# Expert tiles of a mixture-of-experts layer: whole tiles of one expert first, the remainders in quarters of tiles on TensorE column groups

## The chip, the core and the metric

The kernel runs on one core of a Trainium2 chip. A core has TensorE (PE in the profile, with its weight loads as PEld), VectorE (DVE), ScalarE (ACT), GpSimd (POOL) and SyncE (SP, which issues most DMAs). The metric is the device time of one execution in microseconds. The kernel before took 489.15 us (median of 12 runs, 488.44 to 491.28).

## What is computed

A layer norm of x [2, 2048, 256] feeds two branches, whose sum is added to x. One is an RWKV-like attention: two projections, a scan over time per channel, an output projection. The other is a mixture of experts: every one of the 4096 tokens goes through a shared expert of width 512 and through the two of eight experts (width 256) that its gate scores highest. All is f32.

```
xn = layernorm(x)
scores = softmax(xn @ gate_w.T + gate_b);  top_w, top_i = top_k(scores, 2)
expert_e(t) = (silu(t @ w1[e].T + b1[e]) * (t @ w3[e].T + b3[e])) @ w2[e].T + b2[e]
y = sum over the 2 chosen e of top_w * expert_e(xn)
z = (silu(xn @ ws1.T + bs1) * (xn @ ws3.T + bs3)) @ ws2.T + bs2
out = x + attention(xn) + y + z
```

## The kernel before

There are 8 chunks of 512 tokens. For each chunk the kernel loads x and norms it (`norm_flow`: statistics on DVE, 1/std on POOL at lines 459 and 460, the scaling on DVE or ACT), turns it on PE (`turn_flow`) and takes the gate's logits (`by_e`, line 502). These logits are computed by four matmuls with 32 weight columns each, one for each 128 tokens; each writes its own 32 partitions of one PSUM bank.

`route_flow` then picks the two experts of each token and gives each of the 8192 (token, expert) pairs a slot: the pairs of an expert stand together, and each expert's stretch is rounded up to whole tiles of 128 slots. Eight experts round up by less than 8 tiles together, so 64 + 7 = 71 tiles are always enough, and 71 are always computed. `scatter_flow` writes the normed rows to their slots in DRAM (`xs_d`) with 64 indirect DMAs from POOL's queue (line 661); before that the whole of `xs_d` is cleared by 18 DMAs (line 426), so that unused slots carry a target out of bounds. Every second scatter also waits for a PE product (`keep_pace`): the one that was planned `PACE` = 4000 ns before it.

A tile (`tile_flow`) then does: the rows are read back in pairs of tiles (line 966, four DMAs) and turned by DVE (line 970); `ph` = rows times w1 and w3 of the tile's expert, 512 columns, two matmuls over the 256 input channels (line 1006); DVE adds the bias (line 1019), ACT takes the silu (line 1024), DVE multiplies (line 1026), PE turns the result (line 1032) and ACT copies it out of PSUM (line 1036); `pos` = that times w2, 256 columns, two matmuls (line 1042); DVE adds b2 (line 1046), and POOL scatters the rows to `ys_d` (line 1051). The expert's number is read from `owner` into a register of PE and of DVE (`find`, line 951), and weights `we` and biases `b13`, `b2` are addressed with it. At the end `collect_flow` reads `ys_d` back and adds the two weighted rows of each token (line 1080).

The other work of PE is the shared expert (`hidden_flow`, line 856; `dense_flow`, line 924) and the attention's projections (`wvp`, `wrp`, line 796). The attention's exponentials (line 759) and the silu of the tiles take different ACT tables, and ACT loads one at each change.

The order of all this is not left to a scheduler: every piece is a Python generator that says how long it expects to hold which engine (`yield on(400, "POOL")`), which events it needs and which rooms (counted buffers) it takes. `Plan.run` plays these against each other once, when the program is built, and emits the instructions in the order that comes out. The chip then runs each engine's instructions strictly in that order, with semaphores between engines. The numbers in `on(...)` cost nothing on the chip; they decide the order alone. `U` is a pool of 32 buffers of 2 KB per partition.

Of the kernel before, what the change touches and what calls it, by code (L numbers as in the profile page):

```python
# [29 lines left out]
F32 = mybir.dt.float32  # L32
# [8 lines left out]
P = 128  # L41
# [154 lines left out]

TILES = 2 * B * T // P + E - 1

# [6 lines left out]

Q = 32

PIECES = (((0,), (1,), (2,), (3,)), ((0, 1), (2, 3)))
NU = 32
KEEP = 3  # L210

PACE = 4000

# [12 lines left out]
def rwkv_moe_kernel(  # L226
# [36 lines left out]
    XST, SIS, HST, Y = Room(plan, 2), Room(plan, 3), Room(plan, 3), Room(plan, 3)  # L263
    STATS = Room(plan, 3)
    ONE = {}
# [21 lines left out]
    part_d = nc.dram_tensor("part_d", [B * T, C], F32, kind="Internal").ap()  # L287
    bias_d = nc.dram_tensor("bias_d", [2 * E * NI, P], F32, kind="Internal").ap()
    xs_d = nc.dram_tensor("xs_d", [TILES * P, R], F32, kind="Internal").ap()

# [33 lines left out]
    def constants():  # L324
        make_identity(nc, ident)
        nc.gpsimd.memset(zero, 0.0)
        nc.gpsimd.memset(neg_half, -0.5)
        nc.gpsimd.memset(ones, 1.0)

        nc.gpsimd.memset(before, 1.0)  # L330
        nc.gpsimd.affine_select(
            out=before, in_=before, pattern=[[1, P]], compare_op=ALU.is_gt, fill=0.0, base=0, channel_multiplier=-1
        )

        for e in range(E):
            nc.gpsimd.memset(rev[:, e : e + 1], float(E - e))

        nc.gpsimd.iota(starts, pattern=[[P, TILES]], base=0, channel_multiplier=0, allow_small_or_imprecise_dtypes=True)
        nc.gpsimd.memset(wg[:, :, E:], 0.0)
        nc.gpsimd.memset(st_pp, -10000.0)  # L340
        nc.gpsimd.memset(st_bb, 0.0)
        nc.gpsimd.memset(st_aa, 0.0)
# [40 lines left out]
    def load_flow():  # L383
# [38 lines left out]
        nc.gpsimd.memset(none[:, :, R_TO], float(4 * B * T))  # L422
        for j in range(0, TILES, NT):
            n = min(NT, TILES - j)
            yield on(900, "SP")
            nc.sync.dma_start(
                xs_d[j * P : (j + n) * P, :].rearrange("(p n) c -> p n c", p=P), none[:, :n, :]
            )
        land(TILES * P * 1024, [have["cleared"]], X)

# [13 lines left out]
    def norm_flow(c, groups):  # L444
# [12 lines left out]
        rstd = two.tile([P, m], F32, tag="rstd", name=f"rstd_{of}")  # L457
        yield on(400, "POOL")
        nc.gpsimd.tensor_scalar(rstd, mv[:, :, 1], EPS, None, ALU.add)
# [68 lines left out]
    def route_flow():  # L528
# [71 lines left out]

        room_i = pool.tile([P, E], I32, tag="room_i", name="room_i")
        nc.vector.tensor_scalar(room_i, each[:, 0, :], float(P - 1), None, ALU.add)
        nc.vector.tensor_scalar(room_i, room_i, 7, 7, ALU.logical_shift_right, ALU.logical_shift_left)
        room = small("room")
        nc.vector.tensor_copy(room, room_i)
        end = small("end")
        nc.vector.tensor_tensor_scan(end, room, zero.to_broadcast([P, E]), 0.0, ALU.add, ALU.add)

        off = small("off")
        nc.vector.tensor_tensor(off, end, room, ALU.subtract)  # L610
        nc.vector.tensor_tensor(off, off, each[:, 1, :], ALU.add)
        nc.vector.tensor_tensor(off, off, upto[:, 2, :], ALU.subtract)
        nc.vector.tensor_tensor(off, off, each[:, 2, :], ALU.add)
        nc.vector.tensor_scalar(off, off, -1.0, None, ALU.add)
        nc.vector.tensor_tensor(run, run, off.unsqueeze(2).to_broadcast([P, E, G]), ALU.add)
        for n, (which, to) in enumerate(zip((one1, one2), slot)):
            yield on(1250, "DVE")
            nc.vector.tensor_tensor(eq, which, run.rearrange("p e g -> p g e"), ALU.mult)
            nc.vector.tensor_reduce(q, eq, AX.X, ALU.add)
            nc.vector.tensor_copy(to, q)  # L620
        have["routed"].set()

        yield on(1700, "DVE")
        past = pool.tile([P, TILES, E], F32, tag="past", name="past")
        nc.vector.tensor_tensor(
            past, end.unsqueeze(1).to_broadcast([P, TILES, E]),
            starts.unsqueeze(2).to_broadcast([P, TILES, E]), ALU.is_le,
        )
        count = small("count", (P, TILES))
        nc.vector.tensor_reduce(count, past, AX.X, ALU.add)  # L630
        nc.vector.tensor_scalar(owner, count, float(E - 1), None, ALU.min)
        nc.vector.tensor_scalar(likes, count, float(E - 1), None, ALU.min)
        nc.vector.tensor_scalar(likes, likes, -1.0, float(E), ALU.mult, ALU.add)
# [15 lines left out]
    def scatter_flow():  # L649
# [5 lines left out]
        for side, chunks in (("left", LEFT), ("right", RIGHT)):  # L655
            for c in chunks:
                for n in range(NT):
                    g = c * NT + n
                    for w in range(2):
                        yield on(1340, "POOL")  # L660
                        step = nc.gpsimd.indirect_dma_start(  # L661
                            out=xs_views[2 * g + w],
                            out_offset=bass.IndirectOffsetOnAxis(ap=slot[w][:, g : g + 1], axis=0),
                            in_=xn[c][:, n, :],
                            in_offset=None,
                        )
                        if w:
                            keep_pace(step)
                land(0, [scattered[c]])
# [6 lines left out]
            else:  # L676
                late["pool3"] = ctx.enter_context(tc.tile_pool(name="late3", bufs=3, side="right"))
                late["poolg"] = ctx.enter_context(tc.tile_pool(name="lateg", bufs=3, side="right"))
        for j in range(TILES):
            plan.add(tile_flow(j), 10 + j / 100)  # L680
        for j in range(0, TILES, 2):
            plan.add(rows_flow(j), 10 + j / 100)
        for j in range(0, TILES, GO):
# [4 lines left out]
    def bias_rows_flow():  # L688
# [8 lines left out]
        yield on(400, "SP")  # L697
        nc.sync.dma_start(bias_d, bt)
        land(0, [have["bias_d"]], U)

    def bias_flow():
        for c in LEFT:
            yield scattered[c]
        yield have["bias_d"]
        for m in range(2):
            yield on(2600, "SP")
            part = bias_d[ts(m, E * NI), :].rearrange("(e i) p -> e (i p)", e=E)
            nc.sync.dma_start(late["b13"][:, :, m, :], part.partition_broadcast(P))
        yield on(2600, "SP")
        nc.sync.dma_start(late["b2"], b_out[:E, :].partition_broadcast(P))  # L710
        land(P * E * 3 * C * 4, [have["bias"]])
# [131 lines left out]
    def hidden_flow(c, i):  # L843
# [3 lines left out]
        if c in LAST:  # L847
            yield turn[TILES - 5]
        pts = []
# [92 lines left out]

    rows_in = {j: event() for j in range(0, TILES, 2)}
    gone = {j: event() for j in range(0, TILES, GO)}
    turned_rows, stored = {}, [0]

    which = {}

    def find(j):

        which[j] = nc.values_load(
            owner[0:1, j : j + 1], engines=[ENG.PE, ENG.DVE], min_val=0, max_val=E - 1,
            skip_runtime_bounds_check_because="a count of experts, held to the last one",
        )

    def rows_flow(j):


        for c in range(NCH):
            yield scattered[c]  # L960
        n = min(2, TILES - j)
        yield on(1500, "SP", (U, 1), (ROWS, 1))
# [4 lines left out]
        yield 3000  # L967
        yield on(620, "DVE", (U, 1), (XST, 1))
        xT = u([P, n, NC, P], f"xsT_{j}")
# [23 lines left out]
    def tile_flow(j):  # L993
        j0 = j // 2 * 2
        yield rows_in[j0]
        xT = turned_rows[j0][0][:, j % 2]
        yield have["we"]
        if j:
            yield turn[j - 1]
        yield on(1740, "PE", (PS, 1), (PH, 1), spare=(PS, 1))  # L1000
        if j == 0:
            find(j)
        ev = which.pop(j)
        ph = bank([P, 2, I], f"ph_{j}")
        for k in range(NC):
            nc.tensor.matmul(  # L1006
                ph, xT[:, k, :], we[:, bass.ds(ev, 1), 0:2, k, :], start=(k == 0), stop=(k == NC - 1)
            )
        if j + 1 < TILES:
            find(j + 1)  # L1010
        turned_rows[j0][1] -= 1
        if turned_rows[j0][1] == 0:
            U.give()
            XST.give()
        turn[j].set()
        yield have["bias"]
        yield on(690, "DVE", (U, 1), (H, 1))
        h = u([P, 2, I], f"h_{j}")
        nc.vector.tensor_tensor(h, ph, late["b13"][:, bass.ds(ev, 1), :, :], ALU.add)  # L1019
        PS.give()  # L1020
# [17 lines left out]
        HP.give()  # L1038
        yield on(880, "PE", (PS, 1), (PO, 1), spare=(PS, 1))
        po = bank([P, C], f"pos_{j}")  # L1040
        for i in range(NI):
            nc.tensor.matmul(po, hT[:, i, :], we[:, bass.ds(ev, 1), 2, i, :], start=(i == 0), stop=(i == NI - 1))  # L1042
        HST.give()
        yield on(420, "DVE", (U, 1), (YS, 1))
        y = u([P, C], f"ys_{j}")
        nc.vector.tensor_tensor(y, po, late["b2"][:, bass.ds(ev, 1), :], ALU.add)  # L1046
        PS.give()
# [180 lines left out]
```

## Time and profile before

| what | value |
|---|---|
| median of 12 runs | 489.15 us |
| the profiled execution: time | 489.38 us |
| the profiled execution: span in the trace | 487.4 us |
| granted TensorE clock over it | 0.995 |
| DVE busy | 394.2 us (81%) |
| ACT busy | 186.9 us (38%) |
| POOL busy | 168.4 us (35%) |
| DMA moved | 77.36 MB, 159 GB/s in the mean |

The page gives busy time for each engine over the span, the chain of work that ended last, and the costliest groups of instructions, with the mean time of one and the idle time ahead of it. A matmul of f32 stands in the trace as two records. The records of matmuls overlap (one shows 595 ns for 512 columns while the next starts 430 ns later), so durations of matmuls are read from the distance of starts and not from the busy time.

### The profile page before, as it was taken

To read this page: it belongs to the slowest core of one execution; us is meant where nothing else is said; L and a number is where in the kernel's file an instruction comes from. 1 tells how busy PE (TensorE), PEld (TensorE's weight loads), DVE (VectorE), ACT (ScalarE), POOL (GpSimd) and SP (SyncE) were. 2 spreads that over 40 slices of the span, in tenths; PEclk is the share of its full clock that TensorE was granted. 3 is DMA by queue.
4 is the path that set the end of the run, shared out by engine and by line. 5 is a ranking of instruction groups with operands and counts; after the bars stand their busy time and mean duration, and the time that the engine had idled before them with its cause. 6 is when DMAs were issued, how large, how long until landed. Compare 5 with 4: busy or idle time off the path is not lost.

```text
span 487.4 us, 6242 instructions
## 1 busy us (share of the span) xinstructions
PE 470.0 (96%) x1683; PEld 278.5 (57%) x1683; DVE 394.2 (81%) x783; ACT 186.9 (38%) x332; POOL 168.4 (35%) x205
## 2 busy tenths in 40 slices
PE   3999999999999899999999999999999999999996
PEld 1555566445776455555655555656555555444885
DVE  4776999887695798999799779997699866978793
ACT  3776311531500166224912295224922277211000
POOL 6540057777785041433223331442233232000000
PEclk9999999999999899999999999999999999999999
DMA  6999998829345777234322432228321210388872
GB/s 206 370 395 402 219 208 326 264 104 341 137 139 178 97 145 160 75 78 102 71 65 76 117 75 65 82 61 217 76 56 48 75 65 2 106 266 267 270 243 101
DMA packets 92097, 77.36 MB, mean 159 GB/s; under 512 B 52989, under 2 KB 79774, under 8 KB 91808
## 3 DMA queue, kind: packets, MB, share of 16 engines
q1 hardware_dynamic: 85584, 60.12, 45.0%
q0 software_dynamic: 6480, 16.85, 9.7%
q8 instruction: 15, 0.25, 0.2%
q14 instruction: 18, 0.15, 0.1%
HBM read 42.31 MB, written 35.54 MB: 160 GB/s over the span
## 4 chain that ended last, share of the span: by engine, by line
PE 75%; ACT 9%; DVE 8%; issue 3%; POOL 2%; DMA 1%; DVEq 0%; SPq 0%; POOLq 0%
PE p L856 20%; PE ph L1006 16%; PE po L924 15%; PE pos L1042 9%; PE wvp L796 6%; PE wrp L796 5%; ACT L1024 3%; ACT L759 3%; PE hsp L1032 2%; POOL rstd L460 2%; DVE h L1019 1%; DVE aa L811 1%; ACT sis L1024 1%; DVE ys L1046 1%; DVE stats L454 1%
## 5 line engine op out<-in xcount | busy, mean ns | idle before, releaser
L1051 POOL DMA_INDIRECT ys_d<-ys,goes x71 | 77.3, 1089 | 186.1 <-DVE ys L1046 164.4
L1006 PE MATMUL ph<-we,xsT 128*128 x284 | 134.7, 599 | 2.2 <-issue 2.2
L856 PE MATMUL p<-xnT,ws 128*128 128x512 f32 x256 | 114.4, 595 | 0.2 <-DMA ws<-in_w_sh_dram 0.2
L661 POOL DMA_INDIRECT xs_d<-xn,slot x64 | 71.1, 1111 | 49.4 <-DMA we<-in_w_exp_dram 27.8
L856 PEld LDWEIGHTS p<-xnT,ws 128*128 128x128 f32 x256 | 48.0, 191 | 55.2 <-issue 51.9
L1006 PEld LDWEIGHTS ph<-we,xsT 128*128 128x128 f32 x284 | 50.7, 192 | 40.9 <-issue 40.0
L1042 PEld LDWEIGHTS pos<-we,hsT 128*128 128x128 f32 x284 | 53.5, 190 | 31.3 <-issue 19.3
L1042 PE MATMUL pos<-we,hsT 128*128 x284 | 70.2, 381 | 0.8 <-ACT hsT L1036 0.8
L1019 DVE TENSOR_TENSOR h<-ph,b 128x512 f32<-128x512 f32 x71 | 48.6, 687 | 15.0 <-PE ph L1006 13.8
L924 PE MATMUL po<-ws,si 128*128 128x256 f32 x256 | 59.2, 379 | 0.0
L1024 ACT ACTIVATE sis<-h 128x256 f32<-128x256 f32 x71 | 29.0, 415 | 70.9 <-DVE h L1019 70.6
L924 PEld LDWEIGHTS po<-ws,si 128*128 128x128 f32 x256 | 48.6, 190 | 10.4 <-issue 3.6
L863 ACT ACTIVATE si<-p,vec 128x512 f32<-128x512 f32 x32 | 21.5, 684 | 60.0 <-PE p L856 60.0
L1036 ACT COPY hsT<-hsp 128x256 f32<-128x256 f32 x71 | 24.4, 368 | 47.5 <-PE hsp L1032 47.5
L1026 DVE TENSOR_TENSOR sis<-sis,h 128x256 f32<-128x256 f32 x71 | 29.1, 414 | 10.8 <-ACT sis L1024 10.5
L1046 DVE TENSOR_TENSOR ys<-pos,b 128x256 f32<-128x256 f32 x71 | 28.6, 414 | 8.1 <-PE pos L1042 5.3
L924 PE MATMUL po<-wo,rw 128*128 128x256 f32 x128 | 31.9, 379 | 0.0
L824 ACT ACTIVATE th<-wrp 128x512 f32<-128x512 f32 x16 | 9.6, 598 | 57.1 <-PE wrp L796 57.1
L796 PE MATMUL wrp<-xnT,wr 128*128 128x512 f32 x64 | 30.1, 592 | 0.0
L970 DVE STREAM_TRANSPOSE xsT<-xs 128x512 f32<-128x512 f32 (+1 forms) x36 | 25.0, 696 | 5.2 <-DMA xs<-xs_d 4.9
L796 PE MATMUL wvp<-xnT,wv 128*128 128x512 f32 x64 | 29.0, 593 | 0.0
L924 PEld LDWEIGHTS po<-wo,rw 128*128 128x128 f32 x128 | 24.3, 190 | 5.9 <-issue 2.6
(128 smaller groups left out, 525.7 us busy)
## 6 DMA issues: line engine op xcount, KB each, us to landing
xs<-xs_d SPq DMA_DIRECT2D x140, 64.0 KB, 2.4
xs_d<-none SPq DMA_DIRECT2D x17, 516.0 KB, 10.4
y<-ys_d SPq DMA_DIRECT2D x32, 256.0 KB, 3.4
xb<-in_x_dram SPq DMA_DIRECT2D x8, 512.0 KB, 4.6
we<-in_w_exp_dram SPq DMA_DIRECT2D x16, 256.0 KB, 10.9
pa<-part_d SPq DMA_DIRECT2D x8, 512.0 KB, 4.7
xn<-in_x_dram SPq DMA_DIRECT2D x14, 256.0 KB, 6.7
part_d<-xb SPq DMA_DIRECT2D x5, 512.0 KB, 3.1
```

The source lines that it names most:

```text
L661: step = nc.gpsimd.indirect_dma_start(out=xs_views[2 * g + w], out_offset=bass.IndirectOffsetOnAxis(ap=slot[w][:, g : g + 1], axis=0), in_ ...
L796: nc.tensor.matmul(pt, wa[name][:, k, ts(ch, P)], xnT[c][k], start=(k == 0), stop=(k == NC - 1))
L856: nc.tensor.matmul(pt, ws13[:, m, k, ts(i, P)], xnT[c][k], start=(k == 0), stop=(k == NC - 1))
L924: nc.tensor.matmul(po[:, j, :], l[:, ts(2 * half + j, P)], r, start=(i == 0), stop=(i == len(parts) - 1))
L970: nc.vector.transpose(xT.rearrange("p n k (b t) -> p n b k t", t=Q), t.rearrange("p (n b) (k i) -> p n b k i", n=n, i=Q))
L1006: nc.tensor.matmul(ph, xT[:, k, :], we[:, bass.ds(ev, 1), 0:2, k, :], start=(k == 0), stop=(k == NC - 1))
L1019: nc.vector.tensor_tensor(h, ph, late["b13"][:, bass.ds(ev, 1), :, :], ALU.add)
L1024: nc.scalar.activation(si, h[:, 0, :], AF.Silu)
L1026: nc.vector.tensor_tensor(si, si, h[:, 1, :], ALU.mult)
L1042: nc.tensor.matmul(po, hT[:, i, :], we[:, bass.ds(ev, 1), 2, i, :], start=(i == 0), stop=(i == NI - 1))
L1046: nc.vector.tensor_tensor(y, po, late["b2"][:, bass.ds(ev, 1), :], ALU.add)
L1051: nc.gpsimd.indirect_dma_start(out=ys_views[j], out_offset=bass.IndirectOffsetOnAxis(ap=goes[:, j : j + 1], axis=0), in_=y, in_offset=None ...
```

## The change

The slots are given out in another way. Each expert first gets its whole tiles: the number of its pairs divided by 128, rounded down. Those of all experts come first. What is left of each expert (under 128 pairs) is rounded up to quarters of a tile (32 slots), and these follow, expert after expert. The first 57 tiles (`UNI`) then can be done like before, as tiles that belong to one expert. The last 9 are `mixed`: each quarter of 32 rows has an expert of its own. Together 66 tiles, not 71.

A mixed tile runs its matmuls per quarter: 32 weight columns (32 rows of the tile), 512 or 256 moving columns, each quarter into its own 32 partitions of the bank, four matmuls where there was one. The moving weights of a quarter are first copied by ACT from `we` to a buffer of its own (`own`, 2 x 512 elements per quarter for w1 and w3, 1 x 512 for w2: 12 copies a tile, 108 in all), with the expert's number in an ACT register (4 loads a tile). The biases are gathered by row with two indirect DMAs from POOL's queue a tile. The mixed tiles do not come last: they are put in at places 20, 25, ... 60 of the order (`SEQ`).

Other edits: routing computes the two sets of stretches (13 more small DVE instructions ahead of the slots, some of 256 elements); only the mixed part of `xs_d` is cleared (3 DMAs, not 18); `bias_d` is laid out by expert; rows of uniform tiles are still read in pairs, of mixed tiles singly; and four planned costs change: the scatter 1340 to 1290, the norm's POOL step 400 to 950 + 150 per group of 128 rows, `PACE` 4000 to 2000, and a planned pause of 5000 ahead of the tiles. 

The core of the diff:

```diff
-TILES = 2 * B * T // P + E - 1
+Q = 32
+PAIRS = 2 * B * T
+UNI = PAIRS // P - (E - 1)
+TILES = -(-(PAIRS // Q + E - 1) // (P // Q))
+START, EVERY = 20, 5
+SEQ = list(range(UNI))
+for m in range(UNI, TILES):
+    SEQ.insert(START + EVERY * (m - UNI), m)
+AT = {j: n for n, j in enumerate(SEQ)}
+TOGETHER = {j: min(2, UNI - j) if j < UNI else 1 for j in [*range(0, UNI, 2), *range(UNI, TILES)]}
-PACE = 4000
+PACE = 2000
...
-        for j in range(0, TILES, NT):
+        for j in range(UNI, TILES, NT):
             n = min(NT, TILES - j)
             yield on(900, "SP")
             nc.sync.dma_start(
                 xs_d[j * P : (j + n) * P, :].rearrange("(p n) c -> p n c", p=P), none[:, :n, :]
...
-        yield on(400, "POOL")
+        yield on(950 + 150 * m, "POOL")
...
+        room_i = pool.tile([P, 2, E], I32, tag="room_i", name="room_i")
+        nc.vector.tensor_copy(room_i[:, 0, :], each[:, 0, :])
+        nc.vector.tensor_scalar(room_i[:, 0, :], room_i[:, 0, :], 7, 7, ALU.logical_shift_right, ALU.logical_shift_left)
+        nc.vector.tensor_copy(room[:, 0, :], room_i[:, 0, :])
+        nc.vector.scalar_tensor_tensor(room_i[:, 1, :], each[:, 0, :], float(Q - 1), room[:, 0, :], ALU.add, ALU.subtract)
+        nc.vector.tensor_scalar(room_i[:, 1, :], room_i[:, 1, :], 5, 5, ALU.logical_shift_right, ALU.logical_shift_left)
...
         nc.vector.tensor_tensor(run, run, off.unsqueeze(2).to_broadcast([P, E, G]), ALU.add)
+        nc.vector.tensor_tensor(both, run, end[:, 0, :].unsqueeze(2).to_broadcast([P, E, G]), ALU.is_ge)
+        nc.vector.tensor_tensor(both, both, further.unsqueeze(2).to_broadcast([P, E, G]), ALU.mult)
+        nc.vector.tensor_tensor(run, run, both, ALU.add)
...
-                        yield on(1340, "POOL")
+                        yield on(1290, "POOL")
...
-        for j in range(TILES):
-            plan.add(tile_flow(j), 10 + j / 100)
+        yield 5000
+        for j in SEQ:
+            plan.add(tile_flow(j), 10 + AT[j] / 100)
...
+    def expert(j, q, engines):
+        return nc.values_load(
+            owner[q * Q : q * Q + 1, j : j + 1], engines=engines, min_val=0, max_val=E - 1, ...
+    def find(n):
+        if n < TILES and SEQ[n] < UNI:
+            which[SEQ[n]] = expert(SEQ[n], 0, [ENG.PE, ENG.DVE])
+
+    def quarters_flow(j):
+        yield have["bias_d"]
+        yield have["we"]
+        yield turn[SEQ[AT[j] - 6]]
...
+        yield on(1300, "POOL", (MIX, 1), (U, NC * len(quarters) + 1), spare=(U, 2))
+        biases("b13", bias_d, 2 * I)
+        for q in quarters:
+            for k in range(NC):
+                yield on(650, "ACT")
+                if k == 0:
+                    which[j, q] = bass.ds(expert(j, q, [ENG.Activation]), 1)
+                mine[q, k] = u([P, 2, I], f"own_{j}_{q}_{k}")
+                nc.scalar.copy(mine[q, k], we[:, which[j, q], 0:2, k, :])
+        own_in[j].set()
+        yield turn[j]
+        MIX.give()
+        yield on(1300, "POOL", (U, len(quarters) + 1), spare=(U, 2))
+        biases("b2", b_out[:E, :], C)
+        for q in quarters:
+            yield on(650, "ACT")
+            mine[q] = u([P, NI, C], f"own2_{j}_{q}")
+            nc.scalar.copy(mine[q], we[:, which[j, q], 2, :, :])
+        own2_in[j].set()
...
         for k in range(NC):
-            nc.tensor.matmul(
-                ph, xT[:, k, :], we[:, bass.ds(ev, 1), 0:2, k, :], start=(k == 0), stop=(k == NC - 1)
-            )
+            for q in range(P // Q) if mixed else ():
+                rows_q = ts(q, Q)
+                nc.tensor.matmul(
+                    ph[rows_q], xT[:, k, rows_q], own[j][q, k], start=(k == 0), stop=(k == NC - 1)
+                )
+            if not mixed:
+                nc.tensor.matmul(ph, xT[:, k, :], we[:, e, 0:2, k, :], start=(k == 0), stop=(k == NC - 1))
```

The second product of a mixed tile (`pos`) is cut into quarters in the same way, and its two bias adds read the gathered rows.

## The prediction

> **What bounds the kernel now.** I read the page's busy times first, then the chain of waits, then the costliest groups.
>
> ```profile
> span 487.4 us, 6242 instructions
> ...
> PE 470.0 (96%) x1683; PEld 278.5 (57%) x1683; DVE 394.2 (81%) x783; ACT 186.9 (38%) x332; POOL 168.4 (35%) x205
> ...
> PE 75%; ACT 9%; DVE 8%; issue 3%; POOL 2%; DMA 1%; DVEq 0%; SPq 0%; POOLq 0%
> ```
>
> PE is busy 96% of the span, and three quarters of the chain that ended last is PE. The 17 us without PE lie in few places: 6 ahead of the first matmul, some 3 up to 15 us (waits for weights), about 1 at 26 us, 2.2 ahead of the first tile, six times about 0.5 where ACT changes between exponentials and silu, and 4 at the end. So the time is PE's stream plus these gaps, and each part of the change is priced as stream or as gap.
>
> What a tile costs is read from starts, in PE's timeline at 203 us (start, duration, engine, line, tiles, count):
>
> ```profile
> 203.81 1.88 PE L1006 MATMUL ph<-we,xsT 128*128 x4
> 205.53 1.03 PE L1042 MATMUL pos<-we,hsT 128*128 x4
> 206.40 0.38 PE L1032 MATMUL hsp<-ident,sis 128*128 128x128 f32 x2
> 206.62 1.88 PE L1006 MATMUL ph<-we,xsT 128*128 x4
> ```
>
> Four records of 512 columns take 205.53 − 203.81 = 1.72 us (0.43 each), pos 0.87, hsp 0.22: from ph to ph 2.81 us.
>
> **1. Five tiles fewer.** 5 × 2.81 = **−14.0**. Their DVE work (5 × 1.86 = 9.3 us), scatters and loads go too, beside PE, for nothing.
>
> **2. Column groups.** A mixed tile gives four products of 32 columns for each one of 128. If they run one after another, ph and pos cost four times as much; if abreast, the same. The row that shows it is by_e, whose four matmuls also have 32 columns each:
>
> ```profile
> 18.25 1.88 PE L856 MATMUL p<-xnT,ws 128*128 128x512 f32 x4
> 20.06 0.64 PE L502 MATMUL by_e<-xnT,wg 128*32 128x128 f32 x16
> 20.64 3.70 PE L856 MATMUL p<-xnT,ws 128*128 128x512 f32 x8
> ...
> 41.07 1.08 PE L502 MATMUL by_e<-xnT,wg 128*32 128x128 f32 x32
> ```
>
> 32 records of 128 columns, at 0.107 us each, would take 3.4 us in a row. They took 1.08: eight rounds of 0.109, and within a round four records start within 20 ns. So the groups run abreast, and I cost a mixed tile's streaming at a whole tile's.
>
> By the Trainium skill (*TensorE: Matmul & The Clock Gate*, "Measured speedup vs the span model") fourfold packing at 512 columns gained 3.07, not 4. By that a mixed tile's 2.57 us of ph and pos would be an estimated 3.35, and nine tiles +7.0 where I have +6.1 below, with no switches counted; the trace's 3.9 is for 128 columns, and no run yet shows 512.
>
> The change of form is not free. The four p records ahead of the block at 20.06 are streamed, at 0.43 each from 18.25, by 19.97; the eight after it end at 24.34, which less one record's 0.59 and seven of 0.43 puts the first at 20.74. Between is 0.77 us, of which the block's four rounds are 0.43. That leaves 0.34 for going in and out. Each mixed tile has two such blocks, ph and pos: 9 × 2 × 0.34 = **+6.1** (from 0, should blocks four times as long hide it, to twice that, should the moving operand of 512 columns be waited for as well).
>
> **3. The first tile.** Scatters must all have landed before tile 0. POOL's timeline, then PE's:
>
> ```profile
> 61.80 1.21 POOL L661 DMA_INDIRECT xs_d<-xn,slot  x1 [27.76 <-DMA we<-in_w_exp_dram]
> 65.74 1.17 POOL L661 DMA_INDIRECT xs_d<-xn,slot  x1 [2.73 <-PE po L924]
> 67.21 1.27 POOL L661 DMA_INDIRECT xs_d<-xn,slot  x1 [0.30 <-issue]
> ...
> 153.54 0.96 POOL L661 DMA_INDIRECT xs_d<-xn,slot  x1 [0.30 <-PE po L924]
> ```
>
> ```profile
> 156.47 1.88 PE L796 MATMUL wrp<-xnT,wr 128*128 128x512 f32 x4
> 160.58 2.38 PE L1006 MATMUL ph<-we,xsT 128*128 x4 [2.23 <-issue]
> ```
>
> The second scatter waited for the PE product that paces it; from there 62 steps of 1.416 us follow nearly without a wait ("issue" 0.30 between them is the engine's own), and the first ph starts 160.58 − 153.54 = 7.04 after the last scatter does. PE stood idle 2.23 for it. In the changed order the product that the second scatter waits for stands one product of 1.71 us later in PE's order (50.6 us of streaming ahead of it, not 48.9), and tile 0 stands 1.7 earlier (139.6, not 141.3). So the scatters start at about 67.4, tile 0 is ready at 67.4 + 62 × 1.416 + 7.04 = 162.2, and PE is there at 156.6: 5.6 of idle time, **+3.3**. Bounds: steps of 1.27, the shortest, would finish 9 us earlier and remove the gap (−2.2); steps of 1.45 add 2 (+5). I keep 1.416, since the slow steps stand beside DVE's scans, which stay. Routing's 13 more DVE instructions (about 2.4 us by the small ones beside them) bring the slots to some 63.9, behind the paced 67.4, so 0; without that cover up to 2.4. The clear falls from 18 DMAs to 3; the scatter's start is set by routing and pace, so 0.
>
> **4. ACT's copies.** A mixed tile takes 12 copies of 512 elements, 108 in all. ACT's nearest rows are xnT's copies of 512 out of PSUM (line 493): two in 1.07, 0.62 for one alone, so each further one 0.48. That is 52 to 67 us on an engine with 187 of 487 busy; in the mean there is room. Not so where the exponentials run:
>
> ```profile
> 284.36 1.28 ACT L1024 ACT_TABLE_LOAD   x1
> 285.65 0.42 ACT L1024 ACTIVATE sis<-h 128x256 f32<-128x256 f32 x1
> 285.97 0.35 ACT L1036 COPY hsT<-hsp 128x256 f32<-128x256 f32 x1
> 286.34 1.28 ACT L759 ACT_TABLE_LOAD   x1
> 287.64 0.63 ACT L759 ACTIVATE e2b<-e2b 128x512 f32<-128x512 f32 x1
> ```
>
> There ACT has no gap, and behind each table load a tile's silu or hsT is queued, for which PE's hsp and pos wait. In the changed order, between the silu of tile 32 and the hsT of tile 35, ACT has two table loads 2.6, eight copies 3.8, an exponential 0.6, three silus 1.1 and four hsT 1.3 = 9.4 us, where PE's order leaves 8.7: a stall of 0.7. The like count gives about 0.5, 0.8 and 0.8 in three other such stretches and nothing in two: **+2.5**. Added to that are 36 register loads on ACT, which no row shows; the nearest is POOL's 0.30 of "issue". If the previous copy covers them, 0; if not, 4 × 0.3 = 1.2 in each of the four stretches, +4.8. I take 0 here, since a copy's cadence (0.48) is longer than 0.30; the bounds of this term are 0 and +7.3.
>
> **5. The norm's order.** Planned costs of the norm move the early turns. The first p can't pass the DMA of ws at 14.29; the gaps of 0.39 and 0.56 at 26 us may close: **−0.5** (−1 to +1).
>
> **6. Hidden.** 18 gathers of about 1.1 us on POOL (35% busy), against five scatters less; behind a gather stand ys scatters, which nobody but the end needs. The gather for b2 is issued after ph and should land some 3.6 us later, needed 5 or more later. Nine single turns (+0.44 each) on DVE against −9.3; eight more loads from SP. After the last tile's start the read of ys is covered as before. If POOL's or SP's cover were gone, one tile's wait of some 1 to 2 us, once or twice.
>
> **Sum:** −14.0 + 6.1 + 3.3 + 2.5 − 0.5 = −2.6. The profiled execution took 489.38 (span 487.4 and 2.0 around it): 486.8. The median of the runs is 0.23 below that execution: **486.5**.
>
> **Rivals.**
> - *The stalls don't come* (scatters and ACT keep pace): −14.0 + 6.1 − 0.5 = −8.4, **480.7**. For it: ACT and POOL are far from full in the mean, and the scatter has steps of 1.27. Against: the count of orders in 3 and 4.
> - *ACT becomes the bound* (slower than before): its register loads are not hidden, and the four stretches at the exponentials cost 2.5 + 4.8 = 7.3. The sum is +2.2: **491.4**. It decides once those stalls exceed 5.1. For it: ACT has no free slot at 281 to 295 us, and each silu there already waits for a table. Against: the loads need not wait for the copy before.
> - *The groups don't run four abreast.* Two abreast would add 2.57 us to each of nine tiles, 23 in all: near **510**. Against it stand the by_e starts within 20 ns. The Trainium skill (*TensorE: Matmul & The Clock Gate*, "The mechanism") has matmuls strictly first in, first out in start and end; by that rule two records of one f32 product next to each other would hold the other groups up.
> - *The change does something else than it says:* 66 and 71 tiles are counts fixed in the program, so this needs no chance.
>
> **Chances.** Forecast, 484 to 489: 0.46. Stalls away, 479 to 483: 0.23. ACT the bound, 489.5 to 496: 0.24. Groups not abreast: 0.03. Others 0.04. The range of 479.5 to 494 leaves out 0.03 below, and above it the upper end of ACT's case and the groups, 0.03 to 0.1 each. 0.2% is 1.0 us, about what a measurement of this kernel can tell: all of the second case and most of the first lie below 488.2 (0.65), the first's upper edge within (0.12), the third and fourth above (0.23).
>
> **What would show it.** Uniform tiles stay at 2.81 from ph to ph. A mixed ph is four rounds of 0.43 with about 0.1 ahead and 0.2 behind it; rounds of 0.86 mean two abreast. The idle time ahead of the first ph is near 5.6 (term 3), or small. PE's gaps ahead of hsp and pos near the exponentials, ended by ACT, grow by 2.5 together, or by 7. ACT is busy 240 to 255 us. I am wrong if PE's gaps stand elsewhere, as behind a POOL gather or a buffer.

## The result, and the profile after

The changed kernel took 484.27 us (median of 7 runs, 483.72 to 485.44) against 489.15: a ratio of 0.9901, 95% interval 0.9891 to 0.9912. That is 4.9 us less, where 2.6 less (486.5) was forecast. The profiled execution took 484.74, with a span of 483.0, 4.4 less than before.

The page of the changed kernel, the lines that answer to those of before:

```profile
span 483.0 us, 6721 instructions
...
PE 462.1 (96%) x1849; PEld 263.4 (55%) x1849; DVE 386.6 (80%) x782; ACT 220.5 (46%) x416; POOL 182.5 (38%) x221
...
PE 83%; ACT 5%; DVE 4%; SPq 3%; DMA 2%; issue 2%; DVEq 0%; ACTq 0%; POOL 0%; POOLq 0%
```

PE still bounds, with more of the chain than before. ACT has 34 us more to do and yet a smaller part of the chain. The groups of ACT's table loads, of before and then of the changed kernel (count, then busy time and mean):

```profile
L759 ACT ACT_TABLE_LOAD x21 | 26.9, 1283 | 0.4
L1024 ACT ACT_TABLE_LOAD x17 | 21.8, 1283 | 0.3
```

```profile
L801 ACT ACT_TABLE_LOAD x14 | 18.0, 1283 | 0.2
L1120 ACT ACT_TABLE_LOAD x11 | 14.1, 1283 | 2.3 <-DMA xs_d<-xn,slot 2.1
```

In the new order the exponentials stand closer together: 13 loads fewer in these two groups and one in a smaller one, 14 x 1.28 = 18 us. Five tiles fewer take off 4 more (a silu of 0.42 and a copy of 0.37 each). The new copies add 55 (ACT is busy 165.0 without them, in e2).

A uniform tile costs what it did. PE's timeline of the changed kernel, from ph to ph 2.80 us:

```profile
177.77 1.88 PE L1100 MATMUL ph<-we,xsT 128*128 x4
179.49 1.03 PE L1146 MATMUL pos<-we,hsT 128*128 x4
180.35 0.38 PE L1128 MATMUL hsp<-ident,sis 128*128 128x128 f32 x2
180.57 0.59 PE L1100 MATMUL ph<-we,xsT 128*128 x1
```

A mixed ph, in the same view: 16 records of 32 columns, from 229.03 to the next start at 230.88 1.85 us, 0.13 more than a uniform one.

```profile
228.50 0.60 PE L1128 MATMUL hsp<-ident,sis 128*128 128x128 f32 x4
229.03 1.92 PE L1096 MATMUL ph<-own,xsT 128*32 128x512 f32 x16
230.88 1.99 PE L1146 MATMUL pos<-we,hsT 128*128 x8
```

The first scatters and the last of the changed kernel in POOL's timeline, then PE's at the first tile:

```profile
66.67 0.96 POOL L699 DMA_INDIRECT xs_d<-xn,slot  x1 [3.66 <-PE p L898]
...
152.09 1.48 POOL L699 DMA_INDIRECT xs_d<-xn,slot  x1 [0.30 <-issue]
```

```profile
154.82 1.03 PE L966 MATMUL po<-ws,si 128*128 128x256 f32 x4
159.81 4.51 PE L1100 MATMUL ph<-we,xsT 128*128 x6 [3.96 <-issue]
```

To see where the 4.4 us lie, I took the starts of all matmul records, counted 0.428 us of streaming for 512 columns (a quarter of that for each of four records abreast), and called idle what exceeds it up to the next start:

| PE's time, us | before | after | difference | forecast |
|---|---|---|---|---|
| streaming | 455.1 | 441.2 | −13.9 | −14.0 |
| changes of form and other small gaps after 200 us | 1.3 | 6.3 | +5.0 | +6.1 |
| idle ahead of tile 0 | 2.4 | 4.1 | +1.7 | +3.3 |
| four slow records behind that gap | 1.7 | 1.7 | 0 | |
| stalls in the first tiles, to 200 us | 0.7 | 4.1 | +3.4 | 0 |
| stalls of 0.2 and more after 200 us | 2.9 | 2.9 | +0.1 | +2.5 |
| idle in the first 60 us | 15.9 | 15.1 | −0.8 | −0.5 |
| slips under 0.04 and the end | 7.5 | 7.5 | 0 | |

The small gaps divide cleanly. Record by record, each of the 18 blocks of 32 columns costs 0.10 ahead of it, 0.14 more than four rounds up to the next start, and another 0.06 (where turns follow) or 0.11 (where other products follow) behind the first record after it: 0.30 or 0.34, 0.33 in the mean, where 0.34 was forecast. The lines above show the dearer kind: 1.85 − 4 × 0.43 = 0.13 for the block, and 232.71 − 230.88 − 8 × 0.216 = 0.10 in the products behind it. For 18 blocks that is 5.9. The row of the table has +5.0, because 0.4 of the 5.9 lies in slips under 0.04, and the other small gaps fell from 1.3 to 0.8.

The row that nobody forecast is the stalls of the first tiles. PE's and DVE's timelines of the changed kernel show the largest:

```profile
171.54 1.88 PE L1100 MATMUL ph<-we,xsT 128*128 x4
174.48 0.41 PE L1128 MATMUL hsp<-ident,sis 128*128 128x128 f32 x2 [1.07 <-DVE sis L1122]
```

```profile
168.28 0.69 DVE L870 TENSOR_TENSOR aa<-aa,e 128x512 f32<-128x512 f32 x1 [0.24 <-issue]
170.27 0.17 DVE L1074 TENSOR_TENSOR meta<-meta,likes 128x8 f32<-128x8 f32 x1 [1.30 <-DMA meta<-xs_d]
...
172.66 0.69 DVE L1113 TENSOR_TENSOR h<-ph,b 128x512 f32<-128x512 f32 x1
```

The ph of the third tile had streamed by 169.8, but its bias add `h` stands in DVE's order behind four small pairs on the tiles' targets (`meta`), and all four wait for their loads. SP issues the loads one after the other at about half a microsecond each, behind the rows of later tiles:

```profile
163.65 3.98 SPq L1051 DMA_DIRECT2D xs<-xs_d  x8
167.68 4.43 SPq L1070 DMA_DIRECT2D meta<-xs_d  x7
```

In the kernel before, DVE never waited for these loads; here it did for 2.3 us. This makes the stall of 1.2 at 174.5 us, and not the whole row. Another 0.9 stands ahead of hsp at 167.6, and 1.5 ahead of two pos at 183.3 and 193.2 us, where ACT changes its table and a tile's hsT is queued behind that. The first of the two, in ACT's timeline:

```profile
181.03 1.28 ACT L801 ACT_TABLE_LOAD   x1
182.32 0.63 ACT L801 ACTIVATE e1b<-e1b 128x512 f32<-128x512 f32 x1
182.86 0.35 ACT L1132 COPY hsT<-hsp 128x256 f32<-128x256 f32 x1
```

My theory was then: the tiles stand too early in the orders of PE and DVE for the time at which the rows land, and this start of the tiles costs some 5 us more than before or 8 in all (4.1 idle, 1.7 slow records, 2.1 at hsp); the copies on ACT cost nothing; the form of 32 columns costs 5. The rival: the copies cost what was forecast, and the stalls come from them.

### The profile page after: what moved, and what is told of

Its sections match the earlier page's. It is cut to its first block, busy times and chain, and to the rows that moved or that the text cites. A ratio compares the mean times of both kernels' runs of the same rounds, so it can differ in the third digit from the quotient of the medians.

```text
span 483.0 us, 6721 instructions
## 1 busy us (share of the span) xinstructions
PE 462.1 (96%) x1849; PEld 263.4 (55%) x1849; DVE 386.6 (80%) x782; ACT 220.5 (46%) x416; POOL 182.5 (38%) x221
## 4 chain that ended last, share of the span: by engine, by line
PE 83%; ACT 5%; DVE 4%; SPq 3%; DMA 2%; issue 2%; DVEq 0%; ACTq 0%; POOL 0%; POOLq 0%
PE p L898 23%; PE po L966 17%; PE ph L1100 14%; PE pos L1146 8%; PE wrp L838 5%; PE wvp L838 5%; PE ph L1096 3%; PE hsp L1128 3%; PE pos L1142 2%; PE tp L504 1%; SPq L1051 1%; ACT L1120 1%; ACT L801 1%; DMA xn<-in_x_dram 1%; DVE h L1113 1%
## 5 line engine op out<-in xcount | busy, mean ns | idle before, releaser
L1159 POOL DMA_INDIRECT ys_d<-ys,goes x66 | 72.4, 1097 | 157.0 <-DVE ys L1152 146.7
L1100 PE MATMUL ph<-we,xsT 128*128 x228 | 109.0, 602 | 4.0 <-issue 4.0
L699 POOL DMA_INDIRECT xs_d<-xn,slot x64 | 69.2, 1081 | 50.5 <-DMA xb<-in_x_dram 28.0
L1146 PE MATMUL pos<-we,hsT 128*128 x228 | 57.9, 385 | 2.9 <-ACT hsT L1132 2.9
L1100 PEld LDWEIGHTS ph<-we,xsT 128*128 128x128 f32 x228 | 40.8, 193 | 36.2 <-issue 35.4
L1113 DVE TENSOR_TENSOR h<-ph,b 128x512 f32<-128x512 f32 x66 | 45.3, 687 | 16.2 <-PE ph L1100 11.4
L1146 PEld LDWEIGHTS pos<-we,hsT 128*128 128x128 f32 x228 | 42.2, 190 | 26.9 <-issue 14.9
L1120 ACT ACTIVATE sis<-h 128x256 f32<-128x256 f32 x66 | 27.2, 416 | 40.9 <-DVE h L1113 40.3
L1027 ACT COPY own<-we 128x512 f32 x72 | 40.3, 617 | 2.2 <-issue 1.4
L1122 DVE TENSOR_TENSOR sis<-sis,h 128x256 f32<-128x256 f32 x66 | 27.0, 414 | 4.2 <-ACT sis L1120 4.1
```

The source lines that it names most:

```text
L699: step = nc.gpsimd.indirect_dma_start(out=xs_views[2 * g + w], out_offset=bass.IndirectOffsetOnAxis(ap=slot[w][:, g : g + 1], axis=0), in_ ...
L1027: nc.scalar.copy(mine[q, k], we[:, which[j, q], 0:2, k, :])
L1100: nc.tensor.matmul(ph, xT[:, k, :], we[:, e, 0:2, k, :], start=(k == 0), stop=(k == NC - 1))
L1113: nc.vector.tensor_tensor(h, ph, b13, ALU.add)
L1120: nc.scalar.activation(si, h[:, 0, :], AF.Silu)
L1122: nc.vector.tensor_tensor(si, si, h[:, 1, :], ALU.mult)
```

## The experiments

**e1, the form.** The two products of a mixed tile as whole ones, everything else in place:

```diff
-            for q in range(P // Q) if mixed else ():
-                rows_q = ts(q, Q)
-                nc.tensor.matmul(
-                    ph[rows_q], xT[:, k, rows_q], own[j][q, k], start=(k == 0), stop=(k == NC - 1)
-                )
+            if mixed:
+                nc.tensor.matmul(ph, xT[:, k, :], own[j][0, k], start=(k == 0), stop=(k == NC - 1))
```

and pos alike.

> Same order, same copies and gathers, but a mixed tile's two products are done as one 128-column product each, with the first quarter's weights (left out: the other three quarters' own experts). If the change of form costs 0.10 on the way in and 0.12 to 0.22 on the way out, 18 times, this is 5.0 us faster than the changed kernel: 479.3. If the form is free and the cost lies in the copies, it stays at 484.3. If 32-column rounds are slower than 128-column ones (fourfold packing gaining 3.07 by the Trainium skill, TensorE: Matmul & The Clock Gate, Measured speedup vs the span model), it would gain 7 more; the trace of the changed kernel shows rounds of 0.43, which speaks against.

480.07 us, ratio 0.982 (0.9807 to 0.9833): 4.0 us less than the changed kernel, 4.7 by the spans. PE's timeline of e1 at the same tile has no gap: ph to pos 1.72, as in a uniform tile.

```profile
228.45 1.88 PE L1095 MATMUL ph<-own,xsT 128*128 128x512 f32 x4
230.17 1.89 PE L1140 MATMUL pos<-we,hsT 128*128 x8
```

The small gaps after 200 us fell from 6.3 to 0.8, and larger stalls rose from 2.9 to 4.0: 1.1 of the 5.5 comes back as waits, since PE is then sooner at the same ACT results. So the form costs 4 to 5 us net. e1 also makes 216 fewer weight loads (PEld x1633, not x1849), so it doesn't tell the change of form from the loads that come with it.

**e2, the copies.** Quarters read `we[:, q, ...]` directly:

```diff
-                mine[q, k] = u([P, 2, I], f"own_{j}_{q}_{k}")
-                nc.scalar.copy(mine[q, k], we[:, which[j, q], 0:2, k, :])
+                u([P, 2, I], f"own_{j}_{q}_{k}")
+                mine[q, k] = we[:, q, 0:2, k, :]
```

> Same order, but the mixed tiles' quarters read fixed experts 0 to 3 straight from the weights: no copies and no register loads on ACT (left out: the tokens' true experts in mixed tiles). If the copies are hidden, as the stalls near the exponentials (2.9 us in both kernels) suggest, it stays within 0.7 us of the changed kernel: 483.6 to 484.3. If the copies cost the 2.5 us forecast, 481.8. If they also cause the new stalls of the first tiles (2.1 us at 166 to 175 us), about 480.

484.66, ratio 0.9909 (0.9894 to 0.9924): no gain at all. The stalls are the same, too. PE's waits of the changed kernel, then those of e2 (us in total, times, longest):

```profile
PE pos L1146 <- ACT hsT L1132: 2.9, 6, 0.8
PE hsp L1128 <- DVE sis L1122: 1.1, 1, 1.1
```

```profile
PE pos L1144 <- ACT hsT L1130: 3.0, 6, 0.8
PE hsp L1126 <- DVE sis L1120: 1.2, 1, 1.2
```

ACT is named as the releaser in both, but not because of the copies. Two of the six waits for hsT are those behind the table loads at 183 and 193 us, of 0.97 and 0.54 counted by starts, the same in e2. At the other four, after 200 us, PE's order has pos directly behind its own hsp, and PE waits for the way through ACT and back. In e2 ACT was free for all four, and in the changed kernel for two of them; one of these, in PE's timeline and then in ACT's:

```profile
320.57 0.38 PE L1128 MATMUL hsp<-ident,sis 128*128 128x128 f32 x2
321.47 1.13 PE L1146 MATMUL pos<-we,hsT 128*128 x4 [0.52 <-ACT hsT L1132]
```

```profile
321.05 0.37 ACT L1132 COPY hsT<-hsp 128x256 f32<-128x256 f32 x1 [1.93 <-PE hsp L1128]
```

So 108 copies and 36 register loads cost nothing that shows, to within the 1 us or so that the two ratios can tell apart, and the rival falls. ACT is busy 165.0 us here and 220.5 in the changed kernel, so they take it 55.5.

**e3, the copies twice.** Each `nc.scalar.copy` of e2's diff is written a second time.

> Same order, every one of the 108 copies made twice (some 57 us more on ACT). If ACT has room beside the copies, only what falls near the exponentials shows: 2 to 8 us more than the changed kernel, 486 to 492. If the present copies are already on the path there (the rival in which ACT is the bound), each further one counts in the four stretches: 4 x 12 x 0.53 = 25 us more, near 510. If nothing shows, ACT is far from the path.

533.43, ratio 1.09 (1.0882 to 1.0918): 49 us more than the changed kernel, where ACT is busy 64 us longer (284.1, not 220.5). Both numbers were too low, and the shape of the cost was another than either said. PE's waits of e3:

```profile
PE pos L1148 <- ACT hsT L1134: 13.8, 12, 2.8
PE hsp L1130 <- DVE sis L1124: 11.4, 12, 2.1
PE pos L1144 <- ACT hsT L1134: 10.4, 7, 4.0
```

and the longest of them, in ACT's timeline and PE's:

```profile
269.63 0.61 ACT L1027 COPY own<-we 128x512 f32 x1
270.27 0.62 ACT L1028 COPY own<-we 128x512 f32 x1
270.80 0.64 ACT L1134 COPY hsT<-hsp 128x256 f32<-128x256 f32 x2
```

```profile
271.22 1.94 PE L1144 MATMUL pos<-own,hsT 128*32 128x256 f32 x16 [4.03 <-ACT hsT L1134]
```

From 263.7 to 270.8 ACT makes twelve copies without a break, with the hsT of two tiles queued behind them, and PE stands 4 us. ACT as a whole was not full: 185 us busy of the 227 between 208 and 435. As I read it, what decides is the length of a run of copies ahead of a tile's silu or hsT, against the time between a tile's hsp and its pos; single copies fit into it, double ones don't. Not all of the 49 us is waiting: PE's granted clock was 0.93 from 260 to 360 us, where the changed kernel has 1.00.

**e8, the mixed tiles closer together.** `START, EVERY = 30, 2`.

> The changed kernel with the mixed tiles at every second place from 30 on, not at every fifth from 20: the same copies in less than half the time. The copies are hidden at every fifth place (leaving them out gained nothing), and doubled they cost 49 us. If what counts is how much ACT work stands between two mixed tiles, then 12 copies of 0.5 us, two silus and hsT of 0.8 and table loads of 2.6 for each exponential on a stretch of two tiles (9 us) fill ACT, and the nine mixed tiles cost 2 to 5 us each: 500 to 525. If the doubled copies cost so much through the full buffers, not through ACT's time, it is near 484 to 490.

520.13, ratio 1.0534 (1.0488 to 1.058), some 31 us over the changed kernel by the ratios. ACT is busy 81 us of 105 between 275 and 380 us, and PE's waits there are again for ACT's results or for what DVE makes of them. That fits the reading that the copies are hidden because the mixed tiles stand 18 to 20 us apart, with 6 us of copies for each. It doesn't prove it: the whole order is another one, the granted clock was 0.86 from 325 to 380 us, and this order was not run without the copies.

**e4, the pace.** `PACE = 4000`; the order is that of the changed kernel.

> Same order, PACE back to 4000: the second scatter waits for the PE product that stands one of 1.71 us earlier. If the scatters' start sets the first tile, they start 1.7 us earlier, the idle time ahead of tile 0 falls from 4.1 to 2.4 and the time to 482.5; a part of the stalls at 166 to 175 may go as well (to 482.0). If later scatters are held by their own pace, or SP's queue or the last landings set the first tile, it stays at 484.3.

483.9, ratio 0.9895 (0.9881 to 0.991), within the noise of the changed kernel, while the idle time ahead of tile 0 fell from 4.1 to 2.4, as expected, and the span by 1.5. The stall at hsp rose from 1.2 to 1.6. So the scatters' start does set tile 0, but the total was left open; e10 takes it further. The 4.1 of the changed kernel is also high for its order: e1, e2 and e9, which have the same order up to there, show 3.5 to 3.7, so the gain ahead of tile 0 is 1.1 to 1.7.

**e5 to e7, on another chip.** There the kernel before took 493.16. Runs e5, e6, e7 and e8 all show PE idle for 2.5 to 8 us in front of po between 126 and 155 us, "issue" in the profile. In e7 ACT and DVE are all but idle then, too (0.7 and 1.1 us busy from 126 to 140), and in e8 wholly so; e7's view of PE's waits has it thus:

```profile
PE po L966 <- issue: 4.7, 6, 1.5
```

The trace doesn't show what PE waited for. A PE that comes late to tile 0 by itself has less to wait for there, so these three don't test what they were made for. e5, the planned pause ahead of the tiles at 20000:

> The changed kernel with a planned pause of 20000 ahead of the tiles, not 5000: tile 0 stands 5.1 us of streaming later in PE's order (144.7, not 139.6), with other work of PE ahead of it. If the new stalls at the start of the tiles (4.1 us ahead of tile 0, 1.7 for the four slow records behind that gap, 2.1 at hsp behind late target loads) come only from the tiles being put too early, all three go and nothing comes back, since PE's stream is the same: 484.3 - 7 = 477. If the work put ahead is missed later as cover (a gap comes back elsewhere), 480 to 484. If the stalls at hsp are an order of DVE and SP that goes along with the tiles, they stay: 478.5.

492.5, but from 481.75 to 496.32, with a granted clock between 0.979 and 0.995: too wide to read a gain from, so there is no ratio. It was repeated as e11. e6, the kernel before with `yield on(950 + 150 * m, "POOL")` in the norm:

> The kernel before with the norm's planned POOL cost of the changed kernel (950 + 150 per group) and nothing else. If the gaps up to 60 us (15.9 us before, 15.1 after) fell through the norm's order, the kernel is 0.8 us faster than before: 488.4. In this order the product that paces the second scatter stands at 47.2 us of streaming, not 48.9, so the first tile may also gain 1.7: 486.7. If the norm's order does nothing, 489.2.

494.0, ratio 1.0022 (1.0001 to 1.0044). That is no gain, where 0.8 was looked for. PE's idle time in the first 60 us was 14.6, against 15.9; but profiles with the changed kernel's early order gave 14.6 (e9) to about 16.5 (e12). The term of the norm can't be told from the spread of its own stretch. e7, the targets' instructions later in DVE's order (`yield 9000` for `yield 4000` in `goes_flow`):

> The changed kernel with the planned wait for the loads of the targets (meta) at 9000, not 4000: DVE's small instructions on them stand later in its order, behind the first tiles' bias adds. If DVE's wait for these loads (2.3 us at 170 to 173 us, with the bias add of the next tile queued behind) makes the stalls of 0.9 and 1.2 at hsp, they go and the time falls by 1.2 to 2.1: 482.2 to 483.1. If the stalls come from the rows being late, they stay: 484.3.

486.78, ratio 0.9854 (0.9828 to 0.988), 2.3 us below the changed kernel by ratios, and DVE no longer waits for meta; but there is no gap ahead of tile 0 either, because PE came late. It is not a proof.

**e9 to e12, together on a third chip.** e9 is the changed kernel again.

> The changed kernel itself, beside the three others on their chip. On the chip of the runs e5 to e8 the kernel before took 493.2, and PE stood idle for 2 to 9 us at 127 to 155 us, in front of po, with every input long ready. If that is the chip's, it shows here as a ratio off 0.990; else 484.3.

484.79, ratio 0.9913 (0.9892 to 0.9934). e10 has `PACE = 8000`:

> Same order as the changed kernel, only the scatters' waits: the second waits for the PE product at 43.8 us of streaming, not 50.6, so only for its slots. If the scatters' start sets tile 0, they start 3 to 4 us earlier (62.5 to 63.7) and the gap ahead of tile 0 falls from 4.1 to at most 1.0; the four slow records behind it may go with it: 479.5 to 481 against 484.3. If PACE 4000 gave only 0.4 us because something else gives the time back, it stays at 483 to 484.

481.47, ratio 0.984 (0.9816 to 0.9865), 3.6 us below e9. PE's timeline of e10:

```profile
156.86 3.67 PE L1100 MATMUL ph<-we,xsT 128*128 x8 [0.93 <-issue]
160.37 1.88 PE L838 MATMUL wrp<-xnT,wr 128*128 128x512 f32 x4
164.72 0.63 PE L1128 MATMUL hsp<-ident,sis 128*128 128x128 f32 x4 [2.47 <-issue]
```

The gap ahead of tile 0 went from 3.5 to 1.1, and the slow records are gone; but hsp of the first tiles now stands 2.6, not 1.1. Part of the gain is given back one step later, because DVE's order, too, has later rows ahead of the multiply that hsp needs:

```profile
163.51 0.70 DVE L1055 STREAM_TRANSPOSE xsT<-xs 128x512 f32<-128x512 f32 x1
164.13 0.71 DVE L1122 TENSOR_TENSOR sis<-sis,h 128x256 f32<-128x256 f32 x2
```

In e4 only 0.3 is given back so (0.8 and 1.6 at the two hsp, not 0.9 and 1.2).

e11 repeats e5, the pause at 20000:

> As for e5: if the stalls at the start of the tiles come only from tiles put too early in PE's order, 477 on a chip where the kernel before takes 489 (ratio 0.976); if PE is idle elsewhere instead, 480 to 484. On the chip of e5 its one undisturbed run was 481.75 against 493.2, a ratio of 0.977.

481.84, ratio 0.9852 (0.9827 to 0.9877): 3.0 below e9, not 7. PE and DVE of e11 at the first tile:

```profile
157.07 3.60 PE L838 MATMUL wvp<-xnT,wv 128*128 128x512 f32 x8
164.46 7.10 PE L1100 MATMUL ph<-we,xsT 128*128 x16 [3.79 <-issue]
```

```profile
162.15 1.28 DVE L811 TENSOR_TENSOR_SCAN bb<-e1b,bb,e2b 128x512 f32<-128x512 f32 x1
163.47 0.15 DVE L812 COPY st_bb<-bb 128x1 f32<-128x1 f32 x1
163.64 0.71 DVE L1055 STREAM_TRANSPOSE xsT<-xs 128x512 f32<-128x512 f32 x1
```

Tile 0 stands 5 us later in PE's order, and the gap is still there. With so long a pause the plan also put the scan's instructions ahead of tile 0's turn on DVE, and the turn starts at 163.64 although its rows were issued at 156.3. So "too early on PE" was only half of my theory: the orders of PE and DVE must both fit the landing.

e12 changes three numbers of the changed kernel: the pause to 10000, `PACE` to 8000, the targets' wait to 9000.

> Three edits of the order alone: pause 10000 (tile 0 at 141.3 us of streaming), PACE 8000 (scatters 3 to 4 us earlier), targets' wait 9000. If the start of the tiles costs the changed kernel 4.1 of idle time, 1.7 of slow records and 2.1 of stalls at hsp, and nothing comes back, 476.5. If only the idle time goes, 479 to 480.

477.48, ratio 0.9762 (0.974 to 0.9783), 7.4 us below e9 and the fastest of all. PE's timeline of e12 at the first tile:

```profile
157.16 1.88 PE L838 MATMUL wrp<-xnT,wr 128*128 128x512 f32 x4
158.87 5.31 PE L1100 MATMUL ph<-we,xsT 128*128 x12
164.73 0.41 PE L1128 MATMUL hsp<-ident,sis 128*128 128x128 f32 x2 [0.55 <-issue]
```

No gap ahead of tile 0 and no slow records, and DVE doesn't wait for meta; stalls up to 200 us are 3.2 in all, where e9 has 4.4 of them behind 3.5 of idle time and 1.6 of slow records. The profiled execution of e12 was its slowest (479.69), with 2.0 us more idle time in the first 60 us than e9's, so the spans differ by 4.4 only. How much of the gain is the targets' and how much the pause was not tried apart.

## Why the prediction was right, and where it was not

The direction and the range (479.5 to 494) held; the size, 2.6 us, was half of what came. That it came so near is in part luck: misses of −5.5 and +3.4 us offset each other. Term by term:

1. *Five tiles fewer, −14.0:* −13.9 of streaming. A uniform tile stayed at 2.80.
2. *Column groups, +6.1:* right in mechanism and in price: 0.33 a block and 5.9 in the trace. What is left of it in the time is 4.0 to 4.7 (e1), since some of it covers waits. The groups run fully four abreast at 512 columns: the rounds follow one another at 0.43, as whole records do. The estimate from the Trainium skill (*TensorE: Matmul & The Clock Gate*, "Measured speedup vs the span model", where the 3.07 of 4 is for four row groups, and three column groups have 2.38), +7.0 with no changes of form counted, does not hold here: the rounds cost nothing, and the whole price is the change of form.
3. *First tile, +3.3:* measured +1.7. The second scatter started at 66.67, not 67.4, since PE's first 60 us were 0.8 shorter; and a step took (152.09 − 66.67) / 62 = 1.378, not 1.416, 2.4 us over the row. From the last scatter to ph it took 7.7, not 7.0. Other profiles of the same order have 3.5 to 3.7 of idle time, not 4.1, so the term is +1.1 to +1.7. The link from pace to scatter to idle time is confirmed by e4 and e10. The routing got 12 more DVE instructions, 8 of them ahead of the slots, and not 13 ahead of them; the pace covered them, as taken.
4. *ACT's copies, +2.5:* this step failed. Its four parts add up to 2.8, not 2.5, and the copies measured 0 (e2). I counted the work of ACT in a stretch against PE's, and took the difference for a stall; but the copies fit into the time in which ACT waits for PE. I also misread the stalls of about 0.5 in the kernel before: only three of the six (at 294, 351 and 407 us) stand behind a table load; in the other three ACT had been idle for over 3 us before the tile's silu. Waits behind table loads made 1.7 us before (0.3 at 182 us among them) and 1.5 after, so they did not "grow by 2.5 together". ACT was busy 220.5 us, not 240 to 255, as I took the table loads as they were; 14 of 44 went with the new order, and gave ACT back a third of what the copies take. The rival built on it, "ACT becomes the bound", names a real mechanism at the wrong load: it showed at twice the copies (e3), and perhaps at under half the distance (e8). The register loads were hidden, as taken.
5. *The norm's order, −0.5:* −0.8 in the trace, within the spread of that stretch (14.6 to 16.5 for one early order); not settled.
6. *Hidden:* gathers, single turns and SP's loads cost PE nothing that shows, with one exception that I missed. SP's queue at the first tiles makes the targets late, and DVE's order puts them ahead of a bias add: 1.2 of the stalls up to 200 us, which grew by 3.4. I priced SP's loads in sum, and not at the one moment when they all are issued at once. Of the rest, 1.5 are the table loads of term 4, moved to this place, and the 0.9 ahead of the first hsp was not traced to one cause. I had written that I am wrong if PE's gaps stand elsewhere; in this part they did.

By the rows of the table the misses were −1.1 (of which the blocks themselves are only −0.2), −1.6, −2.5, −0.3 and +3.4, together −2.1: from −2.6 to −4.7, near the measured −4.6 of the two profiled executions (489.38 to 484.74). The rival "the stalls don't come" (480.7) was right on ACT and wrong on the start of the tiles; with the start mended, e12 gives 477.5.

## What to carry to other kernels

Where the emission order is planned ahead, look at the moment when a new phase begins: every queue (PE, DVE, SP) has its own order there, one late landing is paid on each in turn, and moving one queue alone gives part of the time back on the next (3.6 us gained in e10, 3.0 in e11), while moving them together gained 7.4 (e12). In such an order, put other work between an instruction and the one that needs its result by way of another engine: pos directly behind its hsp cost 0.4 to 0.7 us, four times, as much with ACT free (e2) as with copies on it. Extra work on an engine with spare time cost nothing here where each uninterrupted run of it was shorter than the slack of the instruction queued behind it, and most of its length beyond that (49 of 64 us in e3), so space it out. A change of matmul form is paid per block and not per column (0.34 at 512 columns, at 256, and at 128 in by_e, with two-record products behind it); keep blocks long or next to each other.

## What the runs showed of the hardware

Behind the gap ahead of tile 0, four of PE's records took 0.86 us and not 0.43: the first four in the changed kernel, and those from 161.9 us on, 1.4 us behind the gap, in the kernel before. The granted clock was 0.52 from 159.8 to 163.3 us in the changed kernel and 0.66 from 160.6 to 164.9 in that of before. It is not the length of the gap alone: 2.4 us brought it on in the kernel before and in e4, 1.1 us in e10 didn't, and neither did the 3.8 us in e11 (granted clock 1.00 behind it). The Trainium skill (*TensorE: Matmul & The Clock Gate*, "Why this matters for your kernels") warns of gaps over some 3 us; here the shorter gap lost the clock and the longer one did not.

The traces show what decided it. The clock falls to 0.50 for 3.41 us or a multiple of it, and in one trace these stretches start a whole number of 3.41 us apart (159.94 and 484.21 in the changed kernel, 95 of them). Laid out in such steps, a fall from the full clock came behind every step in which PE was idle for more than 0.64 of the time, and behind none with less than 0.61, over all 14 traces from 20 us on; between the two both occur. In the kernel before, all but 0.4 us of the gap lies in the step from 158.56 to 161.97, idle for 0.62, and the next step has 0.50. In e11 an edge at 162.49 cuts the gap into two steps idle for 0.58 and 0.60, and the clock stays. That was luck: its three other executions had a mean clock of 0.991 to 0.993, not 1.00, and took 0.5 to 1.2 us longer.

A copy of 512 elements takes 0.62 alone and, in an unbroken run, 0.52 (three in 1.64): 55.5 us of ACT's time for 108, inside the 52 to 67 that was estimated from the copies out of PSUM.
